# Reordering one step of a two-direction state-space scan: exponentials, mask, sum of states and row statistics change places

## The chip, the cores and the metric

The kernel runs on one core of one Trainium2 chip. The metric is the device time of one execution in microseconds (us), the median of several runs. The core has four compute engines that work side by side, each through its own instructions in order: TensorE (PE, matrix products; its weight loads are listed as PEld), VectorE (DVE), ScalarE (ACT, table functions) and GpSimd (POOL). SyncE (SP) issues DMA transfers. An engine that waits for another one holds back everything that stands behind the waiting instruction in its own queue.

## The reference, cut to what matters

Three layers follow each other on an input of 4 images, 128 channels, 64x64 points:

1. a convolution block with a non-local attention (7x7, 5x5 and 3x3 convolutions, attention over 4096 points, relu);
2. a Mamba-like mixer, run forwards and backwards over the 4096 tokens of each of the 4 sequences, after a layer norm of each token's row;
3. a recurrence over tokens, after another layer norm and a batch norm.

The change lies in the second. With x the normalised tokens, for each direction:

```python
z, xbc, dt = split(x @ in_proj)                  # 256, 256 + 64 + 64, 4 columns
xbc = silu(conv(xbc, 4 taps) + conv_b)           # causal, one filter per channel
xh, B, C = split(xbc)                            # 4 heads of 64, states of 64
dt = softplus(dt + dt_bias);  A = -exp(A_log)
y = ssd(xh, dt, A, B, C) + xh * D                # scan over chunks
yg = y * silu(z)
out = (yg * rsqrt(mean(yg * yg) + eps) * norm_w) @ out_proj
# result: x + out of the forward and of the backward direction
```

ssd works by chunks of tokens. Inside a chunk, each pair of tokens l >= s adds (C_l . B_s) * exp(cs_l - cs_s) * dt_s * xh_s, where cs is the running sum of dt*A; a state of 64x64 per head carries the rest from chunk to chunk, faded by exp of the chunk's total.

## The kernel before, in words

The function `mamba` (from line 895) handles 4 sequences of 32 steps: 128 steps of 128 tokens each, both directions in one step (the forward chunk from the front, the backward chunk from the back). Four steps make a group of 512 tokens; `j` is the step's place in its group (0 to 3), `at` its place in its sequence (0 to 31), `n` its number over all. Everything in float32.

The order of the work is written out by hand: PE, ACT, DVE and POOL carry out their instructions in the order of the code (`manual_schedule`, line 996). SyncE's transfers are ordered by the framework's planner, which also chooses which of the buffers of a tag a tile gets. The pieces that the change and the prediction touch, in the order of a step n (lines 1455 to 1540):

- `states` (1244): 4 small matmuls give the state that step n adds, into the PSUM tile `small`; DVE adds the carried, already faded state (line 1260). This is the **sum of states**, S.
- `scan` (1263) and `carried` (1275): 32 small matmuls write the output of step n into the PSUM tile `y`, from the weighted tokens and from the state in front.
- `open_step(n+3)` (1421): SP loads the running sums of step n+3, spread over the partitions, into a `lt` tile (one transfer, three buffers) and its exponentials into a `ct` tile (two transfers).
- `mask(n+2)` (1174): two POOL instructions put 1e30 where the pair of tokens is not causal.
- `reads(n+1)` and `fade(n+1)` (1230, 1235): POOL multiplies `ct` by C and fades the state.
- `likeness(n+1)` (1204): 8 matmuls C.B into `small`, the tile that S is read from as well. `weigh(n+1)` (1225): DVE multiplies `lt` by it.
- `turn(n+1)` (1190): PE transposes the tokens and B (`ptr`, `pbt`). `tokens(n+1)` (1215): ACT copies `pbt` to `bt`, DVE makes `xdtd` and `xdt`. `take` (1287), on odd steps: DVE reads `y`.
- one piece of `opening` (the next sequence's row statistics, scaling and `steps`) and of `ending` (row statistics of the sequence in front, for the third layer). A piece of row statistics is 4 transposes `ls_in`, 9 DVE instructions and a POOL power (`rsqrt`, line 74).
- the group's stage, by j. j=0: POOL gates (`gate`, 1307), squares of the group in front (ACT 1313, POOL 1316), and for the next group `project` (1129), B, `project`. j=1: squares, `project`, C, `means` (1318: PE `pm`, DVE `ms`, two small transfers). j=2: ACT silu of x (1150), `project_fwd`, `project_z`, `roots` (POOL power of `col`, a small transfer, and the `rs` transfer of 512 KB). j=3: `project_z`, gates, `back` (1381: PE `po` for each direction, DVE rs*po, POOL adds to t).
- `decays(n+2)` (1183): 8 ACT exponentials on `lt`, at the very end of the step.

`project` is a matmul `px`, a DVE memset, an ACT Identity with the first tap (1140), from the second group of a sequence on a 3-column DVE add of the neighbour group's edge (1144), and 3 DVE taps that read `px` (1146). `px`, `pb`, `pz`, `po`, `pm`, `pbt` and `ls_in` share one ring of 3 PSUM buffers, so each of them waits until an older one has been read. ACT loads a function table each time it goes from Exp to Silu and back; Copy, Square and Identity need none.

Of the kernel before, what the change touches and what calls it, by code (L numbers as in the profile page):

```python
# [10 lines left out]
F32 = mybir.dt.float32  # L11
AF = mybir.ActivationFunctionType
# [64 lines left out]
def row_statistics(nc, k, ps, tag, pool, src, mr, parts=None):  # L77

    for j in range(mr.shape[1] // GT) if parts is None else parts:
        pt = ps.tile([P, GT, P], F32, tag=tag, name="ls_in")  # L80
        st = pool.tile([P, GT, nc.vector.BN_STATS_DIM], F32, tag="ls_st", name="ls_st")
        for i in range(GT):
            nc.tensor.transpose(pt[:, i, :], src[:, ds(j * NC + i * P, P)], k.ident)
        for i in range(GT):
            nc.vector.bn_stats(st[:, i, :], pt[:, i, :])  # L85
        for i in range(GT):
            nc.vector.bn_aggr(mr[:, j * GT + i, :], st[:, i, :])
        v = mr[:, bass.ts(j, GT), 1]
        nc.vector.tensor_scalar(v, v, LN_EPS, None, ALU.add)  # L89
        rsqrt(nc, k, v, v)  # L90
        yield


def row_scales(nc, k, ps, tag, pool, src, mr, mem, parts=None):
# [799 lines left out]
def mamba(nc, tc, k, a, t, B, T, vec, first=None, after=None, mr=None):  # L894
# [16 lines left out]
    with ExitStack() as ctx:  # L911
# [97 lines left out]
        def steps(b, tl):  # L1009
# [34 lines left out]
            yield  # L1044
            nc.scalar.activation(e, x, AF.Abs)
            nc.scalar.activation(e, e, AF.Exp, scale=-1.0)
            u, um = pair("u")
            nc.vector.tensor_scalar(u, e, 1.0, None, ALU.add)
            nc.vector.tensor_scalar(um, u, 1.0, None, ALU.subtract)
            nc.vector.tensor_tensor(um, e, um, ALU.subtract)  # L1050
            yield
            nc.scalar.activation(e, u, AF.Ln)
            nc.vector.reciprocal(u, u)
            nc.vector.tensor_tensor(um, um, u, ALU.mult)
            nc.vector.tensor_tensor(e, e, um, ALU.add)
# [70 lines left out]
                product(px, w[0]["x"][:, tap, :], tl[:, rows(g, 0, tap)], tap == 0, tap == KC - 1)  # L1126
            nc.scalar.activation(gr["x"][0][:, 0, :], px, AF.Silu, bias=w[0]["cb"][:, 0:1])

        def project(gr, i, c):


            tl, g = gr["tl"], gr["at"][1]
            px = ring.tile([P, MG], F32, tag="big", name="px")
            wx = w[1]["x"][:, bass.ts(c, P)] if i else w[0]["x1"]
            product(px, wx, tl[:, rows(g, i, PAD)])
            x = gr["x+"][i][:, c, :]
            taps = w[i]["taps"][:, c, :]
            at = lambda n: x[:, PAD - n : PAD - n + MG] if i else x[:, n : n + MG]
            nc.vector.memset(x[:, 0:PAD] if i else x[:, MG:], 0.0)
            nc.scalar.activation(at(0), px, AF.Identity, scale=taps[:, PAD:KC], bias=w[i]["cb"][:, c : c + 1])  # L1140
            if g:
                v = x[:, MG:] if i else x[:, 0:PAD]
                past = groups[gr["at"][0] * NG + g - 1]["x+"][i][:, c, :]
                nc.vector.tensor_tensor(v, v, past[:, 0:PAD] if i else past[:, MG:], ALU.add)
            for n in range(1, KC):
                nc.vector.scalar_tensor_tensor(at(n), px, taps[:, PAD - n : KC - n], at(n), ALU.mult, ALU.add)

        def activate(gr, i, c):
            x = gr["x"][i][:, c, :]
# [40 lines left out]
        def turn(m):  # L1190
# [10 lines left out]
            m["pbt"] = ring.tile([P, P], F32, tag="big", name="pbt")  # L1201
            nc.tensor.transpose(m["pbt"], gr["bc"][0][:, bass.ts(i % MT, P)], k.ident)

        def likeness(m):

            Bs, Cs = (m["g"]["bc"][c] for c in range(2))
            at = m["i"] % MT * P
            for h in range(2):
                for d in range(ND):
                    nc.tensor.matmul(  # L1210
                        p_g[HALF[h], d, :], Bs[HALF[d], ds(at + h * DS, DS)], Cs[HALF[d], ds(at, P)],
                        start=True, stop=True,
                    )

        def tokens(m):

            m["bt"] = wk.tile([P, P], F32, tag="bt", name="bt")
            nc.scalar.copy(m["bt"], m["pbt"])
            for name in ("dtd", "dt"):
                m[name] = wk.tile([P, ND, NHEAD, HD], F32, tag="x" + name, name="x" + name)  # L1220
                nc.vector.tensor_tensor(
                    m[name], m["xh"], m["b"][name][:, :, m["i"], :].unsqueeze(3).to_broadcast([P, ND, NHEAD, HD]), ALU.mult
                )
# [94 lines left out]
        def means(gr):  # L1318


            pm = ring.tile([P, MG], F32, tag="big", name="pm")
            for d in range(ND):
                nc.tensor.matmul(pm[HALF[d]], mean, gr["z"][d][:, 0, :], start=True, stop=True)  # L1323
            ms = wk.tile([P, MG], F32, tag="row", name="ms", bufs=3)
            nc.vector.tensor_scalar(ms, pm, RMS_EPS, None, ALU.add)
            n = ND * MG // P
            m1 = dram.tile([P, n], F32, tag="m1", name="m1")
            nc.sync.dma_start(m1.rearrange("(d q) n -> d (q n)", d=ND), ms[::HD])
            gr["col"] = wk.tile([P, n], F32, tag="col", name="col")
            nc.sync.dma_start(gr["col"], m1)  # L1330
# [119 lines left out]
        open_step(2)  # L1450
        mask(m[1])
        decays(m[1])
        fade(m[0], None)
        S, y = None, None
        for n in range(N):
            G, j = divmod(n, MT)
            b, g = divmod(G, NG)
            gr = groups[G]
            last = g == NG - 1
            more = G + 1 < NGR  # L1460
            at = n % NT
            if at == 0:
                S = None
            S1 = states(m[n])
            if n % 2 == 0:
                y = ps.tile([P, ND, 2, 2 * P], F32, tag="y", name="y")
            scan(m[n], y, S)
            carried(m.pop(n), y, S)
            S = S1
            if j == 0 and more:  # L1470
                open_group(G + 1)
            if n + 3 < N:
                open_step(n + 3)
            if n + 2 < N:
                mask(m[n + 2])
            if n + 1 < N:
                reads(m[n + 1])
                fade(m[n + 1], None if at == NT - 1 else S)
                likeness(m[n + 1])
                weigh(m[n + 1])  # L1480
            if at == 4:
                opening = open_sequence(b + 1) if b + 1 < B else iter(())
            if at == 5:
                ending = ended(b - 1) if after is not None and b > 0 else iter(())
            if n + 1 < N:
                turn(m[n + 1])
                tokens(m[n + 1])
            if n % 2:
                take(gr, j, y)
            turns = 4 <= at < 4 + NT // GT  # L1490
            if turns:
                run(islice(opening, 1))
            if at >= 5 and at % 2:
                run(islice(ending, 1))
            if mr is not None and b == B - 1 and at in (24, 25, 28, 29):
                if at == 24:
                    own = row_statistics(nc, k, ring, "big", wk, t[:, b * T :], mr, (3, 4, 2, 5, 1, 6))
                next(own)
            if j == 0:
                if G > 0:  # L1500
                    gate(groups[G - 1], 3, range(ND))
                    squares(groups[G - 1], (0,))
                if more:
                    project(groups[G + 1], *STEPS_X[0])
                    project_bc(groups[G + 1], 0)
                    project(groups[G + 1], *STEPS_X[1])
            elif j == 1:
                if G > 0:
                    squares(groups[G - 1], (1,))
                if more:  # L1510
                    project(groups[G + 1], *STEPS_X[2])
                    project_bc(groups[G + 1], 1)
                if G > 0:
                    means(groups[G - 1])
            elif j == 2:
                if more:
                    for i, c in STEPS_X:
                        activate(groups[G + 1], i, c)
                    project_fwd(groups[G + 1])
                for i in range(1 if more else ND):  # L1520
                    for c in range(2):
                        project_z(gr, i, c)
                if G > 0:
                    roots(groups[G - 1])
            elif j == 3:
                gate(gr, 1, range(1))
                if more:
                    for c in range(2):
                        project_z(gr, 1, c)
                gate(gr, 1, range(1, ND))  # L1530
                if not more:
                    gate(gr, 3, range(ND), True)
                    squares(gr, (0,))
                if G > 0:
                    back(groups.pop(G - 1))
            if n + 2 < N:
                decays(m[n + 2])

            if at >= 4 and not turns:
                run(islice(opening, 1))  # L1540
        squares(gr, (1,), True)
# [275 lines left out]
```

## Time and profile before

| what | value |
|---|---|
| time, median of 3 runs | 3179.12 us (3177.51 to 3181.69) |
| profiled execution | 3181.99 us, of which the span of the profile is 3180.3 us |
| PE busy in the span | 2808.9 us, 88% |
| DVE, ACT, POOL busy in the span | 70%, 57%, 60% |
| first step to last in the mixer | 1670 to 3014 us of the span |
| mean granted TensorE clock | 0.957 |

The profile's engine times are sums over the whole span, through three layers with different limits. The change concerns the 1344 us of the 128 steps alone, so the lines that matter are those of this window: the share of each engine in it, the table of who waited for whom in it, and the timeline of single steps.

### The profile page before, as it was taken

What the parts mean: (1) busy time and instruction counts of PE and PEld (TensorE: products, weight loads), DVE (VectorE), ACT (ScalarE), POOL (GpSimd) and SP (SyncE); (2) the same over time, 40 slices, a digit from 0 to 9 for tenths busy, and PEclk for the clock granted to TensorE, in tenths of its full rate; (3) what the DMA queues carried; (4) which work ended last, traced back from release to release, by engine and by line L of the source; (5) the groups of instructions that cost most, each with busy time, mean ns of one, the idle gap of its engine ahead of it and who ended that gap; (6) DMA issues with size and microseconds to landing.
All of it is one profiled execution on the core that took longest, in us unless ns stands there. A gap on an engine that the chain in (4) does not pass through costs nothing. (4 is left out here: it accounts for less than half of the span.)

```text
span 3180.3 us, 55073 instructions
## 1 busy us (share of the span) xinstructions
PE 2808.9 (88%) x21335; PEld 1437.3 (45%) x21335; DVE 2225.9 (70%) x3333; ACT 1813.8 (57%) x3070; POOL 1905.6 (60%) x1710
## 2 busy tenths in 40 slices
PE   5799999999999999999978888888788888888876
PEld 1344444455444454444434444444344444444445
DVE  6876668777687767878756765676657665676667
ACT  3343444543444435435437777777677777777756
POOL 4158458566584765765824665566556664556644
PEclk9899999999999999999989999999999999999988
DMA  5310101001010011110042333434333332333332
GB/s 187 124 38 31 38 31 52 16 28 45 23 52 23 29 38 38 37 46 21 23 133 78 88 112 93 95 83 113 72 96 91 111 94 73 95 90 91 84 108 107
DMA packets 108444, 224.94 MB, mean 71 GB/s; under 512 B 25678, under 2 KB 29390, under 8 KB 106764
## 3 DMA queue, kind: packets, MB, share of 16 engines
q1 hardware_dynamic: 96588, 177.53, 20.0%
q10 hardware_dynamic: 11584, 43.78, 4.0%
q8 instruction: 170, 2.79, 0.4%
q14 instruction: 102, 0.84, 0.1%
HBM read 200.83 MB, written 20.44 MB: 70 GB/s over the span
## 5 line engine op out<-in xcount | busy, mean ns | idle before, releaser
L480 DVE TENSOR_TENSOR es<-es,ex 128x1024 f32<-128x1024 f32 x448 | 703.1, 1569 | 83.0 <-ACT ex L463 42.4
L463 ACT ACTIVATE ex<-pf 128x1024 f32<-128x1024 f32 x512 | 497.9, 1022 | 401.7 <-PE pf L461 367.0
L461 PE MATMUL pf<-theta,phi 64*64 64x512 f32 x4096 | 496.0, 598 | 19.6 <-ACT ex L463 19.3
L473 PE MATMUL acc<-ex,gT 64*64 64x512 f32 x4096 | 485.1, 594 | 9.6 <-ACT ex L463 9.6
L1188 ACT ACTIVATE lt<-lt,cs 128x128 f32<-128x128 f32 x1024 | 313.2, 388 | 2.8 <-POOL lt L1178 1.3
L1228 DVE TENSOR_TENSOR lt<-lt,small 128x1024 f32<-128x1024 f32 x128 | 156.3, 1221 | 224.9 <-ACT lt L1188 177.8
L367 PE MATMUL pm<-yf,wt 128*128 128x256 f32 x1152 | 287.6, 382 | 15.9 <-DVE es L486 11.5
L473 PEld LDWEIGHTS acc<-ex,gT 64*64 64x64 f32 x4096 | 158.1, 134 | 298.4 <-issue 285.4
L461 PEld LDWEIGHTS pf<-theta,phi 64*64 64x64 f32 x4096 | 146.8, 133 | 312.5 <-issue 212.1
L367 PEld LDWEIGHTS pm<-yf,wt 128*128 128x128 f32 x1152 | 212.6, 189 | 99.3 <-issue 44.4
L1114 PE MATMUL pb<-tl,wbc_fwd 128*64 128x512 f32 x512 | 247.9, 629 | 6.5 <-DVE ls_st L85 6.5
L1114 PE MATMUL pb<-tl,wbc_bwd 128*64 128x512 f32 x512 | 248.3, 629 | 0.0
L410 ACT ACTIVATE eo<-pm 128x256 f32<-128x256 f32 x88 | 33.8, 384 | 368.0 <-PE pm L367 368.0
L337 POOL TENSOR_TENSOR yf<-yd 128x272 f32<-128x272 f32 x192 | 231.3, 1232 | 1.4
L1178 POOL TENSOR_SCALAR_AFFINE_SELECT lt<-lt 128x512 f32<-128x512 f32 x256 | 156.9, 638 | 47.3 <-DMA lt<-csmem 24.3
L1307 POOL TENSOR_TENSOR yT<-yT,zT 128x512 f32<-128x512 f32 x127 | 160.0, 1276 | 35.0 <-ACT zT L1158 34.5
L1210 PE MATMUL small<-Cst,Bst 64*64 64x128 f32 x1024 | 57.0, 295 | 139.5 <-DVE S L1260 123.9
L337 POOL TENSOR_TENSOR yf<-xp 128x272 f32<-128x272 f32 x128 | 117.9, 952 | 97.5 <-PE pm L367 91.7
L74 POOL TENSOR_TENSOR mr<-mr,neghalf 128x4 f32<-128x4 f32 x64 | 66.9, 1046 | 167.2 <-DVE mr L89 117.1
L1188 ACT ACT_TABLE_LOAD x126 | 161.7, 1283 | 2.3
L1233 POOL TENSOR_TENSOR ct<-ct,Cst 128x512 f32<-128x512 f32 x127 | 162.2, 1277 | 0.0
L1114 PEld LDWEIGHTS pb<-tl,wbc_fwd 128*64 128x64 f32 x512 | 76.0, 149 | 181.4 <-issue 164.2
(293 smaller groups left out, 5831.1 us busy)
## 6 DMA issues: line engine op xcount, KB each, us to landing
lt<-csmem SPq DMA_DIRECT2D x128, 512.0 KB, 5.8
wt<-wd ACTq DMA_DIRECT2D x72, 576.0 KB, 3.7
ct<-csmem SPq DMA_DIRECT2D x256, 128.0 KB, 5.2
rs<-m SPq DMA_DIRECT2D x31, 512.0 KB, 3.8
wd<-t SPq DMA_DIRECT2D x16, 576.0 KB, 3.9
t<-in_x SPq DMA_DIRECT2D x4, 2048.0 KB
rows<-after SPq DMA_DIRECT2D x32, 256.0 KB, 4.7
out<-t SPq DMA_DIRECT2D x4, 2048.0 KB
```

The costliest lines, as they stand in the source:

```text
L337: nc.gpsimd.tensor_tensor(f[:, kx], at(x), at(y), op)
L367: nc.tensor.matmul(pm[:, e, :], wt, src, start=(i == 0), stop=(i == len(terms) - 1))
L461: nc.tensor.matmul(pf[c, e, :], phi[HALF[e], m, c], th[HALF[e]], start=True, stop=True)
L463: nc.scalar.activation(ex, pf, AF.Exp, scale=scale)
L473: nc.tensor.matmul(acc[r][HALF[e]], gT[HALF[r], 2 * m + e, :], ex[HALF[r], e, :], start=(m == 0), stop=(m == NT // 2 - 1),)
L480: nc.vector.tensor_tensor(es, es, ex, ALU.add)
L1114: nc.tensor.matmul(out, w[i]["bc"][:, tap, bass.ts(c, DS)], src, start=(tap == 0), stop=(tap == KC - 1),)
L1178: nc.gpsimd.affine_select(out=v, in_=v, compare_op=ALU.is_ge, fill=1e30, base=0, pattern=[[0, NHEAD], [-step, P]], channel_multiplier=step,)
L1188: nc.scalar.activation(v, v, AF.Exp, scale=-1.0, bias=m["b"]["cs"][:, d, m["i"], h : h + 1])
L1228: nc.vector.tensor_tensor(lt, lt, p_g.unsqueeze(2).to_broadcast([P, ND, NHEAD, P]), ALU.mult)
L1233: nc.gpsimd.tensor_tensor(m["ct"], m["ct"], Cs.unsqueeze(1).to_broadcast([P, NHEAD, P]), ALU.mult)
L1307: eng.tensor_tensor(v, v, gr["z"][d][:, :, half(d, j // 2)], ALU.mult)
```

## The change

It reorders the steps; the arithmetic and its amount stay the same.

- `decays(n+2)` goes from the end of the step to its first half: after `take`, ahead of the stage's work.
- `mask(n+3)` is issued at the end of step n instead of at the beginning of step n+1, ahead of `roots` where j is 2.
- The copy of `pbt` to `bt` goes from `tokens` into `turn`; `tokens` and `take` now follow the pieces of `opening` (where `at` is 4 to 11) and `ending`.
- The edge and the taps of the last `project` of j=0, and the DVE and DMA part of `means` of j=1, are put on a list `held` that runs in the next step, right after `states`, thus after S.
- The POOL power of a piece of row statistics runs at the beginning of the following piece.
- The pieces of `ending` begin at `at` 13 instead of 5.
- `steps` is cut differently: the work after the first exponentials follows one step later, Ln one cut earlier relative to it, and there is one more cut in all.

```diff
         v = mr[:, bass.ts(j, GT), 1]
         nc.vector.tensor_scalar(v, v, LN_EPS, None, ALU.add)
+        yield
         rsqrt(nc, k, v, v)
-        yield
...
             nc.scalar.activation(e, e, AF.Exp, scale=-1.0)
+            yield
             u, um = pair("u")
...
+            nc.scalar.activation(e, u, AF.Ln)
             yield
-            nc.scalar.activation(e, u, AF.Ln)
             nc.vector.reciprocal(u, u)
...
-        def project(gr, i, c):
+        def project(gr, i, c, later=None):
...
+            def rest():
+                if g:
+                    edge()
+                for n in range(1, KC):
+                    nc.vector.scalar_tensor_tensor(at(n), px, taps[:, PAD - n : KC - n], at(n), ALU.mult, ALU.add)
+
+            rest() if later is None else later.append(rest)
...
+            m["bt"] = wk.tile([P, P], F32, tag="bt", name="bt")
+            nc.scalar.copy(m["bt"], m["pbt"])
+
         def likeness(m):
...
         def tokens(m):
-            m["bt"] = wk.tile([P, P], F32, tag="bt", name="bt")
-            nc.scalar.copy(m["bt"], m["pbt"])
...
+            return pm
+
+        def mean_rows(gr, pm):
...
             S1 = states(m[n])
+            for act in held:
+                act()
+            held = []
...
-            if n + 2 < N:
-                mask(m[n + 2])
...
                 turn(m[n + 1])
-                tokens(m[n + 1])
-            if n % 2:
-                take(gr, j, y)
...
-            if at >= 5 and at % 2:
+            if at >= 12 and at % 2:
                 run(islice(ending, 1))
...
+            if n + 1 < N:
+                tokens(m[n + 1])
+            if n % 2:
+                take(gr, j, y)
+            if n + 2 < N:
+                decays(m[n + 2])
...
-                    project(groups[G + 1], *STEPS_X[1])
+                    project(groups[G + 1], *STEPS_X[1], held)
...
-                    means(groups[G - 1])
+                    held.append(lambda gr=groups[G - 1], pm=means(groups[G - 1]): mean_rows(gr, pm))
...
-                if G > 0:
-                    roots(groups[G - 1])
...
-            if n + 2 < N:
-                decays(m[n + 2])
-
+            if n + 3 < N:
+                mask(m[n + 3])
+            if j == 2 and G > 0:
+                roots(groups[G - 1])
             if at >= 4 and not turns:
                 run(islice(opening, 1))
```

More of the change, by code (lines that the diff above doesn't have):

```diff
@@ L1140, in project, with edge @@
             nc.scalar.activation(at(0), px, AF.Identity, scale=taps[:, PAD:KC], bias=w[i]["cb"][:, c : c + 1])
-            if g:
+            def edge():
                 v = x[:, MG:] if i else x[:, 0:PAD]
@@ L1144, in project @@
                 nc.vector.tensor_tensor(v, v, past[:, 0:PAD] if i else past[:, MG:], ALU.add)
-            for n in range(1, KC):
-                nc.vector.scalar_tensor_tensor(at(n), px, taps[:, PAD - n : KC - n], at(n), ALU.mult, ALU.add)
+            def rest():
[4 more added lines that the diff above has]
+            rest() if later is None else later.append(rest)
         def activate(gr, i, c):
@@ L1452, in mamba @@
         decays(m[1])
+        mask(m[2])
         fade(m[0], None)
+        held = []
         S, y = None, None
@@ L1464, in mamba @@
             S1 = states(m[n])
+            for act in held:
+                act()
+            held = []
             if n % 2 == 0:
```

## The prediction, made before the result was known

> **What bounds the kernel now.** I read the busy times first, then the engines within the window of the 128 steps, then who waited for whom in that window, then the timeline of one group.
>
> ```profile
> PE 2808.9 (88%) x21335; PEld 1437.3 (45%) x21335; DVE 2225.9 (70%) x3333; ACT 1813.8 (57%) x3070; POOL 1905.6 (60%) x1710
> ```
> ```profile
> 1670.00:3014.00 1344.00, 1142.71 (x9921) 591.48 (x9921) 865.05 (x1823) 995.82 (x1956) 818.66 (x919) 0.94 0.36 92
> ```
>
> The second line gives, for the steps, busy us of PE, PEld, DVE, ACT, POOL, then the granted clock. PE is busy 85%, ACT 74%. The shortest steps take 8.1 us of pure PE work, 4 x 8.1 = 32.4 per group, and the mean group takes 1344/32 = 42. So some 10 us per group are stalls or half-speed clock (0.06 x 1344 = 81 us of clock in all). The waits in the window:
>
> ```profile
> DVE lt L1228 <- ACT lt L1188: 177.8, 83, 6.9
> ACT bt L1218 <- PE pbt L1202: 171.3, 80, 7.6
> PE small L1210 <- DVE S L1260: 123.9, 43, 8.5
> POOL col L74 <- DMA col<-m: 119.7, 24, 9.8
> POOL mr L74 <- DVE mr L89: 110.3, 28, 6.1
> DVE rs L1386 <- DMA rs<-m: 27.2, 7, 6.2
> ```
>
> PE's own long wait is the third: likeness waits for S, because S stands on DVE behind six taps of j=0. DVE waiting for exponentials is larger but not PE's wait. The timeline of an ordinary group (scan of j=0 starts at 2874.20, next group at 2914.56: 40.36 us; below, times count from 2874.20):
>
> ```profile
> 2886.54 0.45 PE L1210 MATMUL small<-Cst,Bst 64*64 64x128 f32 x8 [2.57 <-DVE S L1260]
> ...
> 2894.23 1.33 PE L1323 MATMUL pm<-zT,mean 128*64 128x512 f32 x3 [1.65 <-POOL zT L1316]
> ...
> 2910.62 1.95 PE L1003 MATMUL po<-yT,wout_fwd 128*64 128x256 f32 x16 [0.83 <-ACT zT L1158]
> ```
> ```profile
> 2904.77 1.28 ACT L1188 ACT_TABLE_LOAD   x1
> 2906.06 2.45 ACT L1188 ACTIVATE lt<-lt,cs 128x128 f32<-128x128 f32 x8
> 2908.42 0.24 ACT L1218 COPY bt<-pbt 128x128 f32<-128x128 f32 x1
> 2908.68 1.28 ACT L1158 ACT_TABLE_LOAD   x1
> 2909.97 1.09 ACT L1158 ACTIVATE zT<-pz 128x512 f32<-128x512 f32 x2
> 2911.08 1.28 ACT L1188 ACT_TABLE_LOAD   x1
> 2912.37 2.44 ACT L1188 ACTIVATE lt<-lt,cs 128x128 f32<-128x128 f32 x8
> ```
>
> The reader should see three PE stalls (S, squares, buffers), and that each step of ACT is copy, table, stage, table, exponentials. After the change it is copy, table, exponentials (together 0.25 + 1.28 + 2.45 = 4.0), table, stage. The same work; but whatever waits for the stage waits about 3.7 us longer after the copy.
>
> **The change, part by part, on this group.** *j=0.* Copy at 2.65. Exponentials end at 6.65, the two squares (1.15) at 7.8, Identity of the first px (0.78) at 8.6, where it ended at 4.63. Edge 0.65, taps 2.33, S 0.41: S ends at 12.05, against 12.29. The held taps leave S's way, but the delayed Identity takes their place: gain 0.25. *j=1.* DVE now has, after S, the held edge and taps 2.95, weigh 1.15, row statistics 1.3, xdtd and xdt 1.2, take 1.56, last edge and taps 2.55, S 0.41: S of j=2 ends at 23.2, against 22.84. Squares, behind exponentials, end at 18.25 instead of 14.84, POOL's add (0.73) at 19.0, so pm can start there, against 20.03 with its wait for the power. Not S: pbt of j=2 follows S by 1.1 and comes at 24.3, against 24.60. *j=2.* On ACT copy, exponentials, table, three silus 1.67, px 0.69, two zT 1.2: 8.85, to 33.2; the next copy follows, 1.0 earlier than before (34.22). *j=3.* Copy to 33.45, exponentials to 37.2, table 38.5, first zT 39.05. The second po needs that ring buffer: 39.05 + 1.75, states 0.43, next group at 41.3 against 40.36: **0.9 slower**. If the planner gives it the first po's buffer instead, rs*po decides: ms moves behind S (23.9 against 22.51, 1.4 later), rs was issued 32.9, lands 3.8 later, with the shift 38.1; rs*po 0.69, po 1.75, states: 41.05. The two ways agree.
>
> The same sum on the quietest group (steps 28 to 31 of the first sequence, 35.1 us; no edges, no row statistics): S 11.4, second S 21.15, copies at 22.3 and 31.15, zT 36.95, next group at 39.1: 4.0 slower. The exponentials of j=3 today fill a gap in which ACT has nothing else to do (po and the next states run on PE); moved, they leave it empty and stand before zT.
>
> *Row statistics.* Before, POOL waits 110.3 + 49.6 us for them with gates and squares behind it; that goes. With `ending` out of steps 5 to 11, the six groups of steps 4 to 11 that also prepare a sequence (42.5, 40.8, 44.2, 44.3, 44.8, 45.1) come to about 41.8 each by the sum above with 0.5 for the extra transposes: -11 in all. The pieces only move to later steps (13 to 31), where a quiet group gets 1.4 more.
>
> *Steps 24 to 27* (51.0, 52.2, 53.7): softplus on DVE (2.4, then 3.6) still stands in front of S, only cut so that it does not wait 2.9 for Ln; the sums by exp move to the end of j=2, behind zT (+4.3). Taken as -1.9 each, bounds -5 and +3.
>
> *Mask.* It holds the same place in POOL's queue (nothing of POOL lies between a step's end and the next step's beginning) except at j=2, where it passes the power that waits for col. Its load is issued after the scan of the same step and lands 5.8 later, at about 7, before the mask. New is that ACT reaches it at 4.2. Today it ends at 6.46 in j=0, after POOL waited 5.28 for row statistics; without that wait my sum has it at 3.35. If it stayed at 6.46, each group would pay 2.3, behind it the whole stage.
>
> *SP.* The small transfers of ms and col come 1.4 later relative to the loads; rs already lands too late 7 times. Bounds: 0 (it is hidden by zT, as above) to 2 us in each of 31 groups, 62. I take 0.
>
> *Edges.* The 3-column add took from 0.15 to 5.82 us; the long ones end when a train of POOL instructions does. I leave their mean unchanged; bounds -18 (all four long ones gone) and +18.
>
> *Clock.* In the group the S stall of 2.57 left the clock at 1.00; in the next, after 2.59, it was 0.74 and the same matmuls took 1.06 instead of 0.59. Afterwards there are two stalls of 2 to 2.7 per group (S, second po) instead of one. By half a slow stretch of 3.4 us more per group the price is 0.85 x 31 = 26; by these rows, where the slow steps were 13.2 against 13.3, nothing, as other waits shrink. I take 0. The Trainium skill's page "TensorE: Matmul & The Clock Gate" (section "HAM oscillation") speaks against the change here: idle gaps beyond about 3.4 us re-throttle PE. No gap in my sum reaches that, so by the page too the term is 0.
>
> The table loads: this trace shows 1.28 and the next activation 0.01 later. The skill's "ScalarE: Activation LUTs" ("What ACT_TABLE_LOAD costs") gives 2.66 with a drain; with that, one more load before zT would cost 1.4 x 31 = 43 more, an estimate from that page. The row decides.
>
> **Sum.** 2 ordinary groups with statistics in the second and third sequence +0.9 each, the last sequence's ordinary ones +4, quiet ones +4.0, +4, +5.4 and +2.2 in the first, its first group +0.8, the last sequence's end +4; six preparing groups -11; steps 24 to 27 -6; first groups of a sequence, scaling and projection groups 0. Together 1.8 + 4 + 15.6 + 0.8 + 4 - 11 - 6 = **+9 us**. In the convolution and the recurrence only the power of the row statistics moves, off every chain that I see: 0. The profiled execution, 3181.99 (span 3180.3 plus 1.7 around it), is 2.9 above the median, 0.1%; the +9 goes on the median, 3188.
>
> **Rivals.** *Forecast:* exponentials ahead of the stage turn the S stall into a zT and DVE stall; 3188, own range 3186 to 3225. *Faster:* zT does not hold the second po, because its buffer comes from elsewhere and rs is on time; then j=3 loses its stall, about 2.2 us in up to 28 groups: 3188 - 62 = 3126 if all, 3153 if a bit more than half. It decides from four or five groups on (9/2.2). For it: the PE wait for zT is only 11 us now, and POOL, free of its waits for statistics, delivers gates and masks earlier. Against: the sum above, by both buffers. *rs late:* ms behind S makes every rs late, 2 us x 31: 3250, with mask or clock similar; for it the 7 late ones today. *Nothing changes:* the gains of statistics and losses of the stage cancel, 3179.
>
> **How the numbers follow.** Chances: forecast 0.38, faster 0.37, rs late (or mask late) 0.14, no change 0.11. A measurement can tell about 0.2%, 6 us. So faster 0.37, same 0.11, slower 0.52. The range 3128 to 3245 reaches to most of both outer cases.
>
> **What would show it.** Right: S's wait on PE falls little and PE's waits for zT rise to 2 us a group; ACT's gap moves to before the copy of j=0; no POOL wait for mr. Wrong: S ends well before 12 in j=0, groups shorter than 40 throughout, or DVE waiting for rs in nearly every group.

## The result, and the profile after

| | before | after |
|---|---|---|
| time, median of 4 runs each | 3178.32 us (3176.30 to 3181.69) | 3221.61 us (3216.66 to 3224.46) |
| profiled execution | 3181.99 us | 3222.92 us |
| 128 steps, first scan to last | 1343.5 us | 1384.0 us |

The changed kernel takes 1.0133 times as long (95% interval 1.0116 to 1.0151): 43 us slower, where the forecast was 9 us slower in a range of 3128 to 3245. The steps hold 40.5 of it.

The busy times of the changed kernel over its span, then the engines within its 128 steps (us, busy PE, PEld, DVE, ACT, POOL, granted clock, DMA share, GB/s):

```profile
PE 2829.7 (88%) x21335; PEld 1454.1 (45%) x21335; DVE 2213.2 (69%) x3333; ACT 1797.6 (56%) x3070; POOL 1904.6 (59%) x1710
```
```profile
1676.00:3060.00 1384.00, 1161.29 (x9928) 607.69 (x9927) 850.24 (x1820) 979.49 (x1955) 817.08 (x917) 0.94 0.34 89
```

PE carries out the same matmuls. Over its own 128 steps (1674 to 3018 us) the kernel before had 1144.8 us of PE busy time, so 16.5 us of the loss are longer matmuls, and the other 24 are PE waiting. The granted clock of the steps is 0.94 before and after, so how much of the 16.5 us is the clock is not shown. The waits within the steps of the changed kernel (engine, line, tile, what ended the wait: us in total, times, longest):

```profile
ACT bt L1212 <- PE pbt L1209: 375.0, 99, 11.7
...
DVE rs L1398 <- DMA rs<-m: 89.2, 18, 10.1
PE small L1220 <- DVE S L1268: 88.9, 45, 6.0
...
PE po L1003 <- DVE rs L1398: 49.1, 10, 7.4
...
PE po L1003 <- ACT zT L1165: 36.5, 20, 2.4
```

Against the lines of before: PE's wait for S fell from 123.9 us, and 15.3 more for the S of each sequence's first step (line 1258), to 88.9. POOL's waits for row statistics (110.3 and 49.6) are gone, and ACT's idle time ahead of its copy doubled, from 171 to 375. New are 49.1 us in which the second po waits for DVE's rs*po, in only 10 groups, and 36.5 instead of 11.1 in which it waits for zT. S 50 us less, po 75 us more: that is PE's 24 us of waiting. The 512 KB load `rs` is late 18 times instead of 7.

The lengths of the groups, from the first scan matmul of one to that of the next, sorted by what else their steps do:

| groups (steps of a sequence) | before | after | after - before | forecast |
|---|---|---|---|---|
| first of a sequence (0-3), first 3 sequences | 122.8 | 119.4 | -3.4 | +0.8 |
| preparing the next sequence (4-11), 6 | 261.7 | 250.6 | -11.1 | -11 |
| ordinary (12-15), 3 | 124.0 | 124.6 | +0.6 | +4.0 |
| scaling (16-19), 3 | 134.1 | 146.8 | +12.7 | 0 |
| projection (20-23), 3 | 124.8 | 140.4 | +15.6 | 0 |
| step sizes (24-27), 3 | 156.9 | 145.6 | -11.3 | -6 |
| quiet (28-31), 3 | 106.5 | 132.4 | +25.9 | +13.4 |
| last sequence, 7 | 287.1 | 298.3 | +11.2 | +8 |

The ordinary group that the prediction replayed (steps 16 to 19 of the last sequence, scan of j=0 at 2910.63, next group at 2950.75) took 40.12 us; PE's waits in it:

```profile
2922.30 0.45 PE L1220 MATMUL small<-Cst,Bst 64*64 64x128 f32 x8 [1.76 <-DVE S L1268]
...
2928.89 1.33 PE L1331 MATMUL pm<-zT,mean 128*64 128x512 f32 x3 [0.40 <-POOL zT L1324]
...
2948.54 1.95 PE L1003 MATMUL po<-yT,wout_bwd 128*64 128x256 f32 x16 [2.00 <-ACT zT L1165]
```

S still stops PE, the squares hardly, and the second po now waits for zT. That is the picture that was forecast, at 40.1 instead of 41.05 to 41.3: the group became 0.2 us shorter, where 0.9 longer was forecast. The quiet groups don't fit it. Their last step (31 of the first sequence) went from 8.9 to 17.9 us. PE, ACT, DVE and SP in it, after the change:

```profile
2010.40 1.90 PE L1003 MATMUL po<-yT,wout_fwd 128*64 128x256 f32 x16
2019.01 3.68 PE L1003 MATMUL po<-yT,wout_bwd 128*64 128x256 f32 x16 [6.71 <-DVE rs L1398]
2022.48 1.07 PE L1258 MATMUL small<-xdtd,bt 128*64 128x256 f32 x4
```
```profile
2010.32 2.44 ACT L1195 ACTIVATE lt<-lt,cs 128x128 f32<-128x128 f32 x8
...
2014.08 1.09 ACT L1165 ACTIVATE zT<-pz 128x512 f32<-128x512 f32 x2
```
```profile
2018.27 0.69 DVE L1398 TENSOR_TENSOR rs<-rs,po 128x512 f32<-128x512 f32 x1 [6.79 <-DMA rs<-m]
```
```profile
2010.34 0.42 SPq L1352 DMA_DIRECT2D rs<-m  x1
```

zT is done at 15.2 (2000 left out), yet the second po starts at 19.0: here it was given the PSUM buffer of the first po, which is free once DVE has multiplied it by rs, and rs, issued at 10.3, is there at 18.3. Both matmul groups behind the gap run at half speed (3.68 for 1.90, 1.07 for 0.60; the granted clock from 2019 to 2022 is 0.50).

Much of these 9 us is not new. Before, rs came as late in this step: DVE got it 8.0 us after its issue at 2005.19, after the change 7.9 us. Both po had their buffers then, but DVE does rs*po ahead of the next S, so PE paid in the step behind:

```profile
2013.16 1.29 DVE L1386 TENSOR_TENSOR rs<-rs,po 128x512 f32<-128x512 f32 x2 [4.42 <-DMA rs<-m]
```
```profile
2014.83 0.63 PE L1210 MATMUL small<-Cst,Bst 64*64 64x128 f32 x8 [4.80 <-DVE S L1258]
```

That next step took 14.1 us before and takes 7.7 now. The three quiet groups, each with the step behind it, went from 149.7 to 155.9 us: 6.2 us more, not 25.9. The rest moved across the border of two rows of the table. Over all steps, PE's waits for an S that stands behind a late rs*po add up to 26.4 us before. After, they are 13.7 us, and the 49.1 us at the second po come on top.

### The profile page after: what moved, and what is told of

Same layout as the page of the kernel before. It is cut to its first block, busy times and chain, and to the rows that moved or that the text cites. A ratio compares the mean times of both kernels' runs of the same rounds, so it can differ in the third digit from the quotient of the medians.

```text
span 3221.1 us, 55129 instructions
## 1 busy us (share of the span) xinstructions
PE 2829.7 (88%) x21335; PEld 1454.1 (45%) x21335; DVE 2213.2 (69%) x3333; ACT 1797.6 (56%) x3070; POOL 1904.6 (59%) x1710
## 5 line engine op out<-in xcount | busy, mean ns | idle before, releaser
L1212 ACT COPY bt<-pbt 128x128 f32<-128x128 f32 x128 | 34.1, 267 | 375.8 <-PE pbt L1209 375.8
L1115 PE MATMUL pb<-tl,wbc_fwd 128*64 128x512 f32 x512 | 236.1, 604 | 2.2 <-DVE xT L1151 1.4
L1115 PE MATMUL pb<-tl,wbc_bwd 128*64 128x512 f32 x512 | 236.9, 605 | 0.0
L1324 POOL TENSOR_TENSOR zT<-zT 128x256 f32<-128x256 f32 x127 | 90.3, 732 | 131.3 <-ACT zT L1321 131.3
L1151 DVE SCALAR_TENSOR_TENSOR xT<-px,taps_bwd,xT 128x512 f32<-128x512 f32 x192 | 144.3, 752 | 27.8 <-ACT xT L1141 17.3
L1003 PE MATMUL po<-yT,wout_bwd 128*64 128x256 f32 x512 | 85.8, 493 | 85.6 <-DVE rs L1398 49.1
```

The source lines that it names most:

```text
L1115: nc.tensor.matmul(out, w[i]["bc"][:, tap, bass.ts(c, DS)], src, start=(tap == 0), stop=(tap == KC - 1),)
```

## The experiments

Each ratio is to the kernel before, in runs on the same chip; 1% is 32 us.

| run | ratio (95% interval) |
|---|---|
| the change | 1.0133 (1.0116 to 1.0151) |
| e1_undo_exp | 0.9813 (0.9788 to 0.9839) |
| e1_only_exp | 1.0333 (1.0314 to 1.0353) |
| e1_undo_mean | 1.0006 (0.9991 to 1.0021) |
| e1_only_stats | 0.9882 (0.9852 to 0.9912) |
| e2_late_j0 | 0.9937 (0.9916 to 0.9958) |
| e2_late_j1 | 1.0075 (1.0046 to 1.0103) |
| e2_late_j3 | 0.9875 (0.9842 to 0.9908) |
| e2_undo_exp_mean | 0.9791 (0.9756 to 0.9826) |
| e3_held_back | 1.0077 (1.0050 to 1.0103) |
| e3_no_taps | 0.9843 (0.9809 to 0.9877) |
| e3_roots_first | 0.9801 (0.9768 to 0.9834) |
| e3_ending5 | 0.9808 (0.9776 to 0.9841) |

The theory: the exponentials ahead of the stage's work cost the time, and the other parts gain. Its rivals: the row chain (ms, col, power, rs) is late because the mean's DVE work stands behind S; or the moved pieces of row statistics collide with that chain.

**e1_undo_exp: the change without the move of the exponentials.**

```diff
             if n % 2:
                 take(gr, j, y)
-            if n + 2 < N:
-                decays(m[n + 2])
...
             if j == 2 and G > 0:
                 roots(groups[G - 1])
+            if n + 2 < N:
+                decays(m[n + 2])
```

> The changed kernel, but with the eight exponentials of a step back at the end of the step, behind the mask and the roots. Theory (exponentials ahead of the stage's work cost the time): the held taps and the delayed power keep their gain of some 15 to 25 us, the quiet groups fall back from 43.9 to about 35 us, the projection groups from 47 to about 43: 3140 to 3165 us, faster than both kernels. Rival 1 (the row chain is late because the mean's DVE work stands behind S): stays at 3205 to 3225 us. Rival 2 (pieces of row statistics and the cut of the step sizes, moved to other steps, collide with the chain): stays near 3215 us.

Measured: 3128.23 us, below what the theory gave. The exponentials cost 1.0133 - 0.9813 = 3.2%, some 102 us. The quiet groups are back at 104.7 us for the three (142.4 with the step behind each, where the kernel before has 149.7), and PE's waits of po for zT and for rs are both gone, with the mean still behind S. A late rs still costs PE 28.7 us through S.

**e1_only_exp: the kernel before with that move alone.** The exponentials stand right behind `take`, which in this kernel is ahead of the pieces of `opening` and `ending`; in the change they come behind these.

```diff
             if n % 2:
                 take(gr, j, y)
+            if n + 2 < N:
+                decays(m[n + 2])
...
-            if n + 2 < N:
-                decays(m[n + 2])
```

> The kernel before with this move alone: the eight exponentials go ahead of the stage's work; mask, held taps, power and pieces stay as before. Theory (exponentials): the squares come 3.7 us later, then pm, ms, and the roots, and S waits for the taps of j=0 as well, which read a px that the delayed Identity holds: 3215 to 3250 us. Rivals 1 and 2: 3170 to 3190 us, as nothing of the mean or of the statistics is moved.

Measured: 3291.97 us, 106 us slower, more than the theory allowed, and about what the other run found from the other side (102). Its 128 steps in the profile (the window first, then waits):

```profile
1679.00:3129.00 1450.00, 1191.47 (x9933) 620.84 (x9931) 845.28 (x1820) 980.22 (x1956) 820.40 (x918) 0.91 0.34 85
```
```profile
PE small L1210 <- DVE S L1260: 158.6, 40, 9.1
DVE xT L1144 <- ACT xT L1140: 153.7, 57, 4.7
...
PE po L1003 <- DVE rs L1386: 24.0, 9, 5.3
```

DVE's add of the edge waits 154 us for the delayed Identity, where it waited 42; S stands behind it, and PE's wait for S rises from 124 to 159. The change holds the last of these taps back until S is done, and has 88.9 there. PE's busy time is 46.7 us above that of before, for the same matmuls, at a granted clock of 0.91 for 0.94: nearly half of the 106 us. The second po waits for rs here too, with the mean where it was before: 24.0 us, where there was no such wait.

**e1_undo_mean: the change with the mean's DVE and DMA part back at j=1.**

```diff
-                    held.append(lambda gr=groups[G - 1], pm=means(groups[G - 1]): mean_rows(gr, pm))
+                    mean_rows(groups[G - 1], means(groups[G - 1]))
```

> The changed kernel with the DVE and DMA part of the mean back at j=1, ahead of S. Theory (exponentials): pm is late by the squares in any case; the mean's two DVE operations come 1 to 1.5 us earlier, S 0.7 later: 3210 to 3225 us. Rival 1 (ms behind S makes rs late): DVE's 89 us of waits for the rs load falls to below 45 and the time to 3180 to 3195 us. Rival 2: no change, 3215 to 3225 us.

Measured: 3188.54 us, the first rival's number. The waits that it named:

```profile
PE po L1003 <- ACT zT L1165: 36.5, 20, 2.4
DVE rs L1398 <- DMA rs<-m: 27.5, 10, 5.8
PE po L1003 <- DVE rs L1398: 17.2, 10, 3.4
```

PE's waits for rs fell from 49.1 to 17.2, those for zT stayed at 36.5 to the digit. The quiet groups take 119.5 us instead of 132.4, the scaling ones 124.7 instead of 146.8. So the theory as put was too narrow: with the exponentials in front, the held mean costs 1.3%.

**e1_only_stats: the kernel before with the delayed power and the later pieces.**

```diff
         nc.vector.tensor_scalar(v, v, LN_EPS, None, ALU.add)
+        yield
         rsqrt(nc, k, v, v)
-        yield
...
-            if at >= 5 and at % 2:
+            if at >= 12 and at % 2:
```

> The kernel before with the delayed power of row statistics and the later pieces of the ending sequence alone. Theory (exponentials): POOL's 160 us of waits for statistics go, the six groups of steps 4 to 11 gain 7 to 11 us, nothing else changes: 3160 to 3175 us. Rival 2 (the moved pieces and the transfer of the row scales collide with the row chain in steps 14 to 23): the scaling and projection groups lose 2 to 6 us each in three sequences: 3190 to 3210 us.

Measured: 3152.59 us, 1.2% faster. By the ratio that is 37 us, where the theory gave 3 to 18 (3175 to 3160 us); what the rest of it comes from was not followed. The second rival falls: this part gains by itself.

**e2_late_j0, e2_late_j1, e2_late_j3: the change, with the exponentials at the end of the step for one j.** For j=3:

```diff
-            if n + 2 < N:
+            if n + 2 < N and not j == 3:
                 decays(m[n + 2])
...
                 roots(groups[G - 1])
+            if n + 2 < N and j == 3:
+                decays(m[n + 2])
```

> The changed kernel with the exponentials at the end of the step in steps of j=0 alone, ahead of the stage in the others. Theory A (each step pays for what stands behind its exponentials; in j=0 it is the Identity of the first project, so its taps and S of j=1): S of j=1 comes some 2.5 us earlier, the mean step of j=0 and j=1 together falls from 20.98 to about 19; 3160 to 3190 us. Theory B (nearly all of the price is in j=3, zT and the second po): 3210 to 3225 us.

> The changed kernel with the exponentials at the end of the step in steps of j=1 alone. Theory A (j=1 pays for its squares, so for pm, and for the third project, so for S of j=2): pm and the taps come about 3 us earlier, DVE's waits for rs fall only a little, as the mean's DVE work stays behind S: 3185 to 3210 us. Theory B (j=3 alone): 3210 to 3225 us.

> The changed kernel with the exponentials at the end of the step in steps of j=3 alone, so that the two zT go first. Theory A: PE's 36.5 us of waits of po for zT go, but rs stays as late as it is and its 49 us of waits remain or grow: 3185 to 3210 us. Theory B (j=3 is nearly all of it): 3130 to 3160 us.

Measured: 3157.55, 3200.16 and 3140.27 us; against the change 62, 18 and 82 us less by the ratios. All three add up to 162, while taking all four moves back is worth 102: the gains overlap, so no share of the 43 us belongs to one j alone. j=3 is the largest, as theory B said, but j=0 is not nothing, as theory A said. j=2 alone was not run. In late_j0 the likeness waits 38 us for S instead of 89, and the projection groups, at 131.5 for 140.4, get most of their loss back, while the quiet ones stay at 131.2.

The same quiet step as above, PE and ACT in late_j3:

```profile
1991.04 1.90 PE L1003 MATMUL po<-yT,wout_fwd 128*64 128x256 f32 x16
1992.77 1.90 PE L1003 MATMUL po<-yT,wout_bwd 128*64 128x256 f32 x16
```
```profile
1990.40 0.60 ACT L1165 ACTIVATE zT<-pz 128x512 f32<-128x512 f32 x1 [0.74 <-PE pz L1003]
1991.26 0.60 ACT L1165 ACTIVATE zT<-pz 128x512 f32<-128x512 f32 x1 [0.26 <-PE pz L1003]
```

The step takes 8.9 us, no po waits, and none runs at half speed: with zT early, the second po takes a buffer that zT has freed. The rs load is no earlier, over all the steps or in this one (the sum of DVE's waits, then DVE and PE):

```profile
DVE rs L1398 <- DMA rs<-m: 89.4, 18, 10.2
```
```profile
1999.13 1.28 DVE L1398 TENSOR_TENSOR rs<-rs,po 128x512 f32<-128x512 f32 x2 [7.01 <-DMA rs<-m]
```
```profile
2000.81 0.71 PE L1220 MATMUL small<-Cst,Bst 64*64 64x128 f32 x8 [4.84 <-DVE S L1266]
```

DVE waits the same 89 us for rs as in the change, and PE pays one step later, as before the change: the step behind takes 15.2 us instead of 7.7, at a granted clock of 0.50 behind its gap. Over all steps PE waits 49.2 us for an S behind a late rs*po, where the change has 13.7 and 49.1 us at po. So the buffer changes the place where PE pays for a late rs, and only part of the price (49.2 for 62.8 us); the quiet groups with the step behind each take 152.5 us for 155.9. The 82 us of late_j3 lie elsewhere: the 36.5 us of po for zT are gone, PE's waits for S in the steps of j=1 fell from 54.9 to 20.9, and PE is busy 21 us less, at a granted clock of 0.96 for 0.94. Why S of j=1 came earlier was not followed. One thing in late_j3 is mixed in: with the exponentials of j=3 and of the next j=0 close together ACT carries out 56 instructions less (3014 for 3070), all of them table loads of 1.28 us. By themselves they decide little: late_j1 has 59 instructions less and gains 18 us.

**e2_undo_exp_mean: both taken back.** The diffs of e1_undo_exp and e1_undo_mean together.

> The changed kernel with the exponentials back at the end of the step and with the mean's DVE and DMA part back at j=1. If the held mean costs by itself (rs late, as the run without it suggests): 3095 to 3118 us. If it costs only behind early exponentials, as pm then comes 3 us earlier and rs has time: 3122 to 3135 us. If it pays without them, by keeping S free: 3138 to 3155 us.

Measured: 3114.2 us, 2.1% faster than before: it beats both kernels. With late exponentials, taking the held mean back is worth 0.2% (0.9813 and 0.9791), and the intervals overlap. The loss of 1.3% that it makes behind early exponentials is not there. The number lies in the bounds of the first expectation, but its distance from e1_undo_exp is within the error, as the second had it; the runs don't separate these two. The traces show a trade: with the mean at j=1, DVE waits for rs only 3 times, and PE's waits for an S behind a late rs*po fall from 28.7 to 2.0 us, while its waits for S in the steps of j=2, where the mean's work then stands ahead of S, rise from 37.9 to 60.7.

**e3_held_back: the change, with DVE's rs*po and POOL's sums in the next step, behind S.** The second po can't be given the first one's buffer then.

```diff
+            both = pos or [outputs(gr, d) for d in range(ND)]
+            def scale():
+                for d in range(ND):
+                    rs = gr["rs"][:, d, :]
+                    nc.vector.tensor_tensor(rs, rs, both[d], ALU.mult)
...
+            scale() if pos else held.append(scale)
```

> The changed kernel, exponentials and mean where the change puts them, but DVE's two products rs*po and POOL's two sums behind them run in the next step, behind S, so that the second po can no longer be given the buffer of the first. Theory (late rs costs only through that buffer): PE's 49 us of waits of po for DVE's rs go, about half comes back as waits of po for zT, the quiet groups fall from 43.9 to about 39.5 us: 3180 to 3198 us. Rival (a late rs stops the step wherever it is read, as DVE has S and the likeness behind it): 3212 to 3230 us.

Measured: 3197.45 us. The time lies at the end of the theory's range; by the ratio, 0.56% below the change, the gain is 18 us, where the theory gave 24 to 42. The waits:

```profile
PE po L1003 <- ACT zT L1165: 60.6, 30, 2.4
DVE rs L1400 <- DMA rs<-m: 11.2, 4, 4.3
```

No wait of po for rs is left, about half of it is back as waits for zT, in 30 groups now. The quiet groups take 39.1, 38.5 and 37.7 us (43.9, 44.7 and 43.9 in the change), and the last step 13.1 instead of 17.9; the step behind does not pay for it (7.8 for 7.7), as S is ahead of rs*po on DVE, and the load has landed by then. The rival's price did not come. Its mechanism is not refuted: where rs*po stands ahead of S, as before and in late_j3, a late rs does stop the next step. The scaling groups stay at 147.6.

**e3_no_taps, e3_roots_first, e3_ending5: the fastest version without one part more.** In the order of the names:

```diff
-                    project(groups[G + 1], *STEPS_X[1], held)
+                    project(groups[G + 1], *STEPS_X[1])
```
```diff
-            if n + 3 < N:
-                mask(m[n + 3])
             if j == 2 and G > 0:
                 roots(groups[G - 1])
+            if n + 3 < N:
+                mask(m[n + 3])
```
```diff
-            if at >= 12 and at % 2:
+            if at >= 5 and at % 2:
```

> Exponentials at the end of the step and mean at j=1, as in the fastest version, and the last project's taps back at j=0 too, so that mask, roots, statistics and cuts alone remain of the change. If the held taps carry what is left of the gain beyond the 34 us of statistics: 3138 to 3155 us. If the mask does: 3106 to 3122 us.

> The fastest version (exponentials at the end of the step, mean at j=1) with the power of the roots ahead of the mask where j is 2. If the mask's place ahead of the roots carries gain, as POOL then waits for col with the mask behind it: 3130 to 3150 us. If it is neutral, as rs stays ahead of what reads it: 3106 to 3122 us. If rs comes earlier and that frees something: below 3105 us.

> The fastest version (exponentials at the end of the step, mean at j=1) with the pieces of the ending sequence back at steps 5 to 15, so that of the statistics only the delayed power and the cut remain. If the gain of the statistics is the power that no longer stops POOL: 3108 to 3125 us. If it is the pieces that leave the steps which prepare a sequence: 3135 to 3150 us.

Measured: 3129.31, 3112.26 and 3114.48 us. The held taps seem to be worth 0.5% (0.9843 against 0.9791, intervals that just overlap; PE's wait for S 113.5 against 73.1 supports it). The mask ahead of the roots and the later pieces are worth nothing that can be told. So what gains in the statistics seems to be the power that no longer stops POOL, by elimination: no run moves the power alone. With the pieces back at steps 5 to 15 the preparing groups take 253.7 us instead of 246.8, and the other groups give that back. These two runs and e2_undo_exp_mean can't be told apart; all three beat both kernels.

## Why the prediction was right in sign and short in size

*The mechanism held where it was worked out.* "Exponentials ahead of the stage turn the S stall into a zT and DVE stall" is what the ordinary group shows: S ends at 11.62 (12.05 forecast), the squares let pm start at 18.26 (19.0), the copy of j=3 comes at 31.92 (33.2), and the second po waits 2.00 for zT. The signs under "What would show it" came for the most part: S's wait at likeness fell by 28% (36% with line 1258), ACT's gap stands ahead of the copy, 191.9 of its 375 us in the steps of j=0, and POOL has no wait for `mr` in the steps. The waits for zT are 1.8 us each, but in 20 groups of 31; and of the signs of being wrong one came by half, DVE waits for rs in 18. Each event of the ordinary group came 0.4 to 1.3 us earlier than summed, so that group became no longer.

*How much was luck.* The sum had 9 of 43 us, in a range 117 us wide, and its largest rival was "faster", at 0.37 against 0.38. The sign rests on zT standing behind the exponentials in j=3, and of the single steps late_j3 does have the largest part. But the scaling and projection groups, taken at 0, hold 28 us of the loss, and the sum saw nothing of them.

*Quiet groups (+13.4 forecast, +25.9 measured): mis-sized, and partly moved.* The steps behind them, which the sum left unchanged, gave 19.7 us back; together it is +6.2. The +4 of zT was about right: without the wait for rs (e3_held_back) they take 37.7 to 39.1 us, and with 2.5 to 3.4 us of it left (e1_undo_mean) 39.0 to 40.6, where the sum had 39.1 for the first. What failed is the step "If the planner gives it the first po's buffer instead, rs*po decides ... The two ways agree". They agree in the ordinary group, for which alone I worked them out, with an rs that "lands 3.8 later". In the quiet one DVE got it 7.9 us after its issue, and 8.0 in the kernel before already; so rs*po starts some 3 us after the zT that I compared it with, and the planner took that buffer there.

*SP (0 taken, bounds 0 to 62): mis-sized.* "rs already lands too late 7 times" had the right signal, and I dismissed it with "hidden by zT". It was not hidden even before: PE paid 26.4 us for it, through S in the step behind. After, it pays 62.8: 49.1 at po, in 10 groups of 0.8 to 7.4 us, not 2 us in 31, and 13.7 through S. e1_undo_mean takes the held mean away and gets 1.3% back; e3_held_back takes the buffer away and gets 0.56% back.

*Scaling groups (0 taken, +12.7): mis-sized, of the same term.* In the groups in front of them (13th to 16th step) the power of col runs 16.1, 16.6 and 18.6 us after the scan of j=2; before it ran at 6.7 to 7.8. SP's queue had a new wait there, and an order that it did not have before (the wait over all steps, then SP in the first sequence):

```profile
SPq L105 <- ACT rs_row L104: 31.8, 3, 11.4
```
```profile
1817.89 4.79 SPq L110 DMA_DIRECT2D tl<-scale  x8
1823.07 0.50 SPq L1340 DMA_DIRECT2D m<-ms  x1
...
1827.26 0.33 SPq L1342 DMA_DIRECT2D col<-m  x1
```

The transfer of the row scales (line 105) waits for ACT, eight loads `tl<-scale` that need it follow, and the small transfers of ms and col stand behind these. I gave every step of the row chain 1.4 us and did not look at what else sits in SP's queue in these steps. The wait for ACT alone is not it: with the mean at j=1 it is 33.6 us, but col goes ahead of at least five of the eight loads, the power runs at 7.6 to 10.0, and the scaling groups take 124.7 us. With late exponentials and the held mean the wait is only 1.7 us, but col still stands behind all eight, and the power is as late (17.0 to 17.6) and these groups as long (146.2). So col is late where it stands behind the eight loads, in all three sequences of each of these runs. That this lateness alone makes the groups longer is not shown: late_j3 has the same order, and they take 136.7 us.

*Projection groups (0 taken, +15.6): mis-sized.* Taking the exponentials back gives 128.5, those of j=0 alone 131.5, the mean alone 144.7. So it is what stands behind the exponentials, mostly in j=0; which of the projection's instructions carries it was not followed further.

*Clock (0 taken, bound +26): open in size.* PE is busy 16.5 us longer, but the granted clock of the steps is 0.94 before and after; the sum's 0 is not refuted. One reason given for it was that no gap would reach the length that matters, and that failed: gaps of up to 7.4 us came, since rs came later than I had it. In the quiet step a gap of 6.71 is followed by matmuls at half speed. In e3_held_back so is one of 2.44; the granted clock is 1.00 up to the end of this gap and 0.50 from 2013.5 to 2016.5:

```profile
2012.85 3.12 PE L1003 MATMUL po<-yT,wout_bwd 128*64 128x256 f32 x16 [2.44 <-ACT zT L1165]
2015.75 1.07 PE L1258 MATMUL small<-xdtd,bt 128*64 128x256 f32 x4
```

The Trainium skill's page "TensorE: Matmul & The Clock Gate" (section "HAM oscillation") puts the limit at gaps of about 3.4 us. The gap of 6.71 us agrees with it; the one of 2.44 doesn't, and the measurement decides: here a gap below that limit was no safe zero.

*Edges (unchanged, bounds -18 and +18):* the mean of the 84 adds fell from 672 to 489 ns, 15 us of DVE's time, near the lower bound; what that is worth to the kernel no run shows. *Preparing groups (-11):* -11.1. *Steps 24 to 27 (-6, bounds -15 and +9):* -11.3; the delayed power and the later pieces alone leave them at 157.1, so it is not these; which part it is was not followed. *Mask:* it kept its place as said, ACT waits 2.2 us for it in all, and where it stands against the roots makes no difference that can be told.

*The rivals.* "Faster" failed by its own condition: zT does hold the second po. "rs late" was right in its cause, the mean behind S, and wrong in its price, 2 us in every group; it came on top of the forecast instead of in its place. By e1_undo_mean it is worth 40 us, which would cover the missing 34; but the projection groups stay long there, so the prices of the parts overlap and can't be added up.

## What to carry to other kernels

Where several consumers share a ring of buffers, work out each buffer that a tile may be given in the group where its release is latest, not in one ordinary group. Then follow a late load to everything that stands behind it: in the same step it cost PE 6.7 us through a buffer after the change, and 4.8 us one step later, through DVE's queue, both before it and in late_j3. The price went away where its reader stood behind the critical result (e3_held_back) or the load came in time (e2_undo_exp_mean). A table by groups can show as a loss what has only moved across a border: add the next step. A change of many parts can hide gains of 2% behind one move that costs 3%: take the moves back one at a time, and two together, since here their prices neither added up nor stayed the same (the held mean cost 1.3% behind early exponentials and 0.2%, within the error, without them). Here the exponentials filled a gap of ACT behind the critical results, and were best left there, though ACT has time to spare.

## What was not expected of the hardware

Slower matmuls can weigh nearly as much as the waits: the kernel with the exponentials alone moved has 46.7 us more PE busy time for the same matmuls, at a granted clock of 0.91 for 0.94, 44% of its loss of 106 us. And a gap of 2.44 us was followed by half-speed matmuls in one place, while the ordinary group's second po ran at its full-speed 1.95 us after a gap of 2.00.
